# Pairwise products of embedding fields on one core: input loads moved into the store queue, output slots of 116 pairs that cross tile boundaries

## The chip, the cores and the metric

The kernel runs on one core of a Trainium2 chip. The metric is the device time of one execution in microseconds (us); for the kernel before, the median of six runs is 1295.54 us (1290.43 to 1296.54).

## The reference

`x` holds 4096 samples of 32 fields with 64 float32 each, `W` is 64 by 64. Every field is multiplied by `W`, and then every pair of fields i < j gives one vector of 64: the raw field i times the transformed field j. There are 496 pairs.

```python
vid = jnp.einsum('bfd,de->bfe', x, W)
idx_i, idx_j = jnp.triu_indices(32, k=1)
return x[:, idx_i, :] * vid[:, idx_j, :]          # (4096, 496, 64)
```

The input is 33.55 MB and the output 520.09 MB.

## The kernel before

The host lays the samples out so that a tile is 256 samples: 128 partitions (two halves of 128 samples, with 64 embedding elements each) by 32 fields by C = 128 samples. There are NT = 16 tiles. A pair is 128 float32 in each partition, so 512 bytes there and 65,536 bytes over all partitions; a tile gives NP = 496 pairs, and all tiles 7936. In HBM the rows of x are padded by 8 fields (PAD), so that one partition's row of 16 KB stands every 20 KB.

For each tile, TensorE multiplies all fields by W (L134, 16 matmuls of two halves and eight PSUM banks) into `vid`, one PSUM tile of 32 fields that fills all eight banks and is used again by every tile. A matmul into a bank therefore waits until VectorE (DVE in the profile) has read the last tile's fields of that bank. VectorE then forms the pairs with one `tensor_tensor` multiplication for each block of pairs (L159): left the field i from `xt` in SBUF, right the field j from `vid`, result into an output slot `ot`. Tiles 0 and 1 go through the pairs field by field (`by_field`: row j needs only the fields 0 to j), all later tiles by larger blocks (`by_block`).

An output slot holds SLOT = 124 pairs (62 KB in each partition), and a tile is four slots exactly. The pool `opool` has three slots. A slot is stored by one DMA when it is full (L162), except in the first two tiles, where the list GROWING cuts the slots into 26 smaller stores, so that the first ones leave early. VectorE writes into a slot again only when all stores of it have landed.

The input pool `xpool` has two places of 16 KB in each partition. Tile 0 is loaded by four DMAs and tile 1 by two, from the queue of SyncE (SP in the profile). Each later tile t + 1 is loaded during tile t by four DMAs of eight fields (4 KB in each partition), from the queue of ScalarE (ACT in the profile), which does nothing else; it waits until tile t - 1 has been used up. Both queues end in the same 16 DMA engines. SP is scheduled by hand (`manual_schedule`): its DMAs are issued in the order in which the program names them, and a DMA that must wait for VectorE holds up those behind it.

Of the kernel before, what the change touches and what calls it, by code (L numbers as in the profile page):

```python
# [1 line left out]

# [4 lines left out]

F32 = mybir.dt.float32
ALU = mybir.AluOpType

P = 128

C = 128

SLOT = 124

PAD = 8

GROWING = [
    21, 15, 19, 23, 27, 19, 29, 18, 19, 20, 38, 28, 24, 25, 47, 34, 29, 61,  # L20
    55, 69, 66, 58, 77, 47, 93, 31,
]


def by_field():

    return [("row", j, 0, 1, j) for j in range(1, 32)]


def by_block():  # L30


    def within(lo):
        yield "step", lo, 2, 1, 0
        for k in range(2):
            yield "step", lo, 4, 2, k
        for i in (lo, lo + 8):
            yield "row", i + 4, i, 4, 4
        yield "row", lo + 8, lo, 8, 8

    yield from within(0)
    yield "row", 16, 0, 16, 16
    yield from within(16)


def products(blocks):

    at = 0
    for kind, a, b, c, d in blocks:

        if kind == "row":
            rows, n, i0, di, j0, dj = c, d, b, 0, a, 1
        else:
            rows, n, i0, di, j0, dj = 16 // b, c, a, b, a + c + d, b
        r = k = 0
        while r < rows:
            room = SLOT - at % SLOT
            if k or room < n:
                m, w = 1, min(n - k, room)
            else:  # L60
                m, w = min(rows - r, room // n), n
            yield at, m, w, i0 + r * di + k, di, j0 + r * dj, dj
            at += m * w
            if w == n or k + w == n:
                r, k = r + m, 0
            else:
                k += w


def pairs(blocks):  # L70

    for at, m, w, i, di, j, dj in products(blocks):
        for r in range(m):
            for k in range(w):
                yield i + r * di + k, j + r * dj


@with_exitstack
def pairwise_bilinear_kernel(
    ctx: ExitStack,  # L80
    tc: tile.TileContext,
    x: bass.AP,
    w: bass.AP,
    out: bass.AP,
):

    nc = tc.nc  # L90
    NT = x.shape[0]
    F = x.shape[2] - PAD
    D = P // 2
    NP = F * (F - 1) // 2

    BANK = 512 // C


    ctx.enter_context(tc.manual_schedule(engines={mybir.EngineType.SP}))

    const = ctx.enter_context(tc.tile_pool(name="const", bufs=1))
    xpool = ctx.enter_context(tc.tile_pool(name="x", bufs=2))
    opool = ctx.enter_context(tc.tile_pool(name="out", bufs=3))
    psum = ctx.enter_context(
        tc.tile_pool(name="ps", bufs=1, space=bass.MemoryType.PSUM)
    )
    vid = psum.tile([P, F, C], F32)


    w2 = const.tile([P, D], F32)  # L110
    nc.sync.dma_start(out=w2, in_=w)  # L111

    def load(t, pieces, queue):
        xt = xpool.tile([P, F, C], F32, tag="x", name=f"x_{t}")
        n = F // pieces
        for lo in range(0, F, n):
            queue.dma_start(out=xt[:, lo : lo + n, :], in_=x[t][:, lo : lo + n, :])
        return xt

    loaded = [load(0, 4, nc.sync), load(1, 2, nc.sync)]  # L120

    done = 0
    growing = iter(GROWING)
    until = next(growing)
    for t in range(NT):
        if 0 < t < NT - 1:
            loaded.append(load(t + 1, 4, nc.scalar))
        xt = loaded[t]


        for b in range(0, F, BANK):
            for h in range(2):
                half = slice(h * D, (h + 1) * D)
                nc.tensor.matmul(  # L134
                    vid[half, b : b + BANK, :],
                    lhsT=w2[half, :],
                    rhs=xt[half, b : b + BANK, :],
                    start=True,
                    stop=True,
                )  # L140

        sent = 0
        for at, m, w, i, di, j, dj in products(by_field() if t < 2 else by_block()):
            base = at - at % SLOT
            if at == base:
                ot = opool.tile([P, SLOT, C], F32, tag="o", name=f"o_{t}_{at}")
            n = m * w
            o = ot[:, at - base : at - base + n, :]
            if m == 1:
                left = xt[:, i : i + w, :]  # L150
                right = vid[:, j : j + 1, :].to_broadcast([P, w, C])
            else:
                o = o.rearrange("p (m w) c -> p m w c", m=m)
                right = vid[:, j : j + (m - 1) * dj + 1 : dj, :].unsqueeze(2).to_broadcast([P, m, w, C])
                if di == 0:
                    left = xt[:, i : i + w, :].unsqueeze(1).to_broadcast([P, m, w, C])
                else:
                    left = xt.rearrange("p (m d) c -> p m d c", d=di)[:, i // di : i // di + m, i % di : i % di + w, :]
            nc.vector.tensor_tensor(o, left, right, ALU.mult)  # L159
            at += n  # L160
            if t * NP + at == until or at in (base + SLOT, NP):
                nc.sync.dma_start(  # L162
                    out=out[t][:, sent:at, :],
                    in_=ot[:, sent - base : at - base, :],
                )
                sent = at
                if t * NP + at == until:
                    until += next(growing, NT * NP)


_INS = ["r_x", "L0_rec_W"]
_OUTS = [((4096, 496, 64), "float32")]


# [36 lines left out]
```

## Time and profile before

| quantity | value |
|---|---|
| median of six runs | 1295.54 us (1290.43 to 1296.54) |
| the profiled execution: its time, its span | 1290.43 us, 1288.5 us |
| VectorE busy | 1083.6 us, 84%, 320 instructions |
| TensorE busy | 229.2 us, 18%, 512 matmuls |
| DMA packets | 20889, with 553.80 MB, mean 430 GB/s |
| DMAs | 82 stores, 62 loads of x, 1 load of W |

The profiled execution is the fastest of the six runs. 1.93 us of its time lie outside its span. DMA rates in the profile count bytes moved by all 16 engines; a share of the span given for a DMA queue is the time that its packets took, averaged over the 16 engines. The median "to landing" of a DMA runs from its issue to its completion, and so it holds the time it stood behind other DMAs.

### The profile page before, as it was taken

To read this page: it belongs to the slowest core of one execution; us is meant where nothing else is said; L and a number is where in the kernel's file an instruction comes from. 1 tells how busy PE (TensorE), PEld (TensorE's weight loads), DVE (VectorE), ACT (ScalarE), POOL (GpSimd) and SP (SyncE) were. 2 spreads that over 40 slices of the span, in tenths; PEclk is the share of its full clock that TensorE was granted. 3 is DMA by queue.
4 is the path that set the end of the run, shared out by engine and by line. 5 is a ranking of instruction groups with operands and counts; after the bars stand their busy time and mean duration, and the time that the engine had idled before them with its cause. 6 is when DMAs were issued, how large, how long until landed. Compare 5 with 4: busy or idle time off the path is not lost.

```text
span 1288.5 us, 1789 instructions
## 1 busy us (share of the span) xinstructions
PE 229.2 (18%) x512; PEld 48.8 (4%) x512; DVE 1083.6 (84%) x320; POOL 0.2 (0%) x4
## 2 busy tenths in 40 slices
PE   4112122122121121221212212122121221212000
PEld 1000000000000000000000000000000000000000
DVE  7999999898898987988879888798887988979870
POOL 0000000000000000000000000000000000000000
PEclk8555556555555555555555555555555555555555
DMA  9999999999999999999999999999999999999998
GB/s 389 428 428 433 439 434 427 436 436 430 432 435 432 421 435 434 431 434 435 431 436 436 430 436 431 428 434 432 434 425 436 437 436 433 433 429 433 438 434 357
DMA packets 20889, 553.80 MB, mean 430 GB/s; under 512 B 2448, under 2 KB 2448, under 8 KB 10256
## 3 DMA queue, kind: packets, MB, share of 16 engines
q1 hardware_dynamic: 12816, 524.33, 94.2%
q10 hardware_dynamic: 8064, 29.36, 5.6%
q8 instruction: 4, 0.07, 0.0%
q14 instruction: 5, 0.04, 0.0%
HBM read 33.59 MB, written 520.09 MB: 430 GB/s over the span
## 4 chain that ended last, share of the span: by engine, by line
DMA 55%; DVE 40%; issue 2%; PE 0%; DVEq 0%; SPq 0%
DMA out_dram<-o 55%; DVE o L159 40%; DMA x<-in_r_x_dram 0%; PE vid L134 0%; DVEq L200 0%; DVEq L159 0%; SPq L111 0%
## 5 line engine op out<-in xcount | busy, mean ns | idle before, releaser
L159 DVE TENSOR_TENSOR o<-x,vid 128x2048 f32<-128x2048 f32 (+13 forms) x320 | 1083.6, 3453 | 165.1 <-DMA out_dram<-o 120.7
L134 PE MATMUL vid<-x,w 64*64 64x512 f32 x512 | 229.2, 1031 | 952.2 <-DMA x<-in_r_x_dram 624.1
L134 PEld LDWEIGHTS vid<-x,w 64*64 64x64 f32 x512 | 48.8, 206 | 1130.9 <-DVE o L159 588.0
L182 POOL MEMSET const-bfloat16-1.0<- 128x1 bf16 x1 | 0.1, 101 | 0.0
L182 POOL MEMSET const-uint8-127<- 128x1 uint8 x1 | 0.1, 101 | 0.0
L182 POOL MEMSET const-float32-0.0<- 128x1 f32 x1 | 0.1, 98 | 0.2 <-issue 0.2
L182 POOL MEMSET const-float32-1.0<- 128x1 f32 x1 | 0.1, 98 | 0.0
## 6 DMA issues: line engine op xcount, KB each, us to landing
out_dram<-o SPq DMA_DIRECT2D x56, 7936.0 KB, 42.9
x<-in_r_x_dram ACTq DMA_DIRECT2D x56, 512.0 KB, 45.1
out_dram<-o SPq DMA_DIRECT2D x2, 3008.0 KB, 17.7
out_dram<-o SPq DMA_DIRECT2D x1, 5952.0 KB, 26.8
out_dram<-o SPq DMA_DIRECT2D x1, 4928.0 KB, 23.1
out_dram<-o SPq DMA_DIRECT2D x1, 4416.0 KB, 19.0
out_dram<-o SPq DMA_DIRECT2D x1, 4224.0 KB, 21.1
out_dram<-o SPq DMA_DIRECT2D x1, 3904.0 KB, 15.3
```

Of the source, the lines that this page charges most:

```text
L134: nc.tensor.matmul(vid[half, b : b + BANK, :], lhsT=w2[half, :], rhs=xt[half, b : b + BANK, :], start=True, stop=True,)
L159: nc.vector.tensor_tensor(o, left, right, ALU.mult)
L182: nc = _bacc.Bacc("TRN2", target_bir_lowering=False, num_devices=1, dynamic_dma_scratch_size=1024)
```

## The change

Loads. All loads of x are issued from SP, so they stand in one queue with the stores. `xpool` has three places. Before the first tile three tiles are loaded: tile 0 by four DMAs as before, tiles 1 and 2 by one DMA each (16 KB in each partition). After every odd tile (1, 3, ... 13) two more tiles are loaded, one DMA each (one tile after 13). ScalarE's queue is not used any more.

Slots. SLOT is 116 pairs (58 KB in each partition), still three slots. They no longer end with a tile: pairs are counted through all 7936, a slot can hold the last pairs of one tile and the first of the next, and the last slot has 48. GROWING covers the first ten slots with 21 stores, the first of 45 pairs. Blocks are cut at the new slot ends, so VectorE has 363 multiplications for 320.

Layout. The output in HBM was (16 tiles, 128 partitions, 496 pairs, 128), so that one partition's row in a tile stands every 248 KiB; it is now (128 partitions, 7936 + 24 pairs, 128), with a row every 3980 KiB.

```diff
-SLOT = 124
-
-PAD = 8
+SLOT = 116
 
 GROWING = [
-    21, 15, 19, 23, 27, 19, 29, 18, 19, 20, 38, 28, 24, 25, 47, 34, 29, 61,
-    55, 69, 66, 58, 77, 47, 93, 31,
+    45, 46, 25, 55, 61, 44, 72, 58, 58, 77, 39, 87, 29, 76, 40, 90, 26, 33,
+    83, 84, 32,
 ]
+
+XPAD = 8
+OPAD = 24
...
-    xpool = ctx.enter_context(tc.tile_pool(name="x", bufs=2))
+    xpool = ctx.enter_context(tc.tile_pool(name="x", bufs=3))
...
-    def load(t, pieces, queue):
+    loaded = []
+
+    def load(pieces=1):
+        t = len(loaded)
+        if t == NT:
+            return
         xt = xpool.tile([P, F, C], F32, tag="x", name=f"x_{t}")
         n = F // pieces
         for lo in range(0, F, n):
-            queue.dma_start(out=xt[:, lo : lo + n, :], in_=x[t][:, lo : lo + n, :])
-        return xt
-
-    loaded = [load(0, 4, nc.sync), load(1, 2, nc.sync)]
+            nc.sync.dma_start(out=xt[:, lo : lo + n, :], in_=x[t][:, lo : lo + n, :])
+        loaded.append(xt)
+
+    load(4)
+    load()
+    load()
...
     for t in range(NT):
-        if 0 < t < NT - 1:
-            loaded.append(load(t + 1, 4, nc.scalar))
         xt = loaded[t]
...
-        sent = 0
-        for at, m, w, i, di, j, dj in products(by_field() if t < 2 else by_block()):
+        for at, m, w, i, di, j, dj in products(blocks(t), t * NP):
             base = at - at % SLOT
...
-            if t * NP + at == until or at in (base + SLOT, NP):
+            if at == until or at in (base + SLOT, NT * NP):
                 nc.sync.dma_start(
-                    out=out[t][:, sent:at, :],
+                    out=out[:, sent:at, :],
...
+        if t % 2:
+            load()
+            load()
...
-        laid = (NT, 2 * D, shape[1], C)
+        laid = (2 * D, NT * shape[1] + OPAD, C)
```

## The prediction

> **What bounds the kernel now.** I began with the page: the busy shares, the slices and the DMA queues.
>
> ```profile
> PE 229.2 (18%) x512; PEld 48.8 (4%) x512; DVE 1083.6 (84%) x320; POOL 0.2 (0%) x4
> GB/s 389 428 428 433 439 434 427 436 436 430 432 435 432 421 435 434 431 434 435 431 436 436 430 436 431 428 434 432 434 425 436 437 436 433 433 429 433 438 434 357
> q1 hardware_dynamic: 12816, 524.33, 94.2%
> q10 hardware_dynamic: 8064, 29.36, 5.6%
> ```
>
> The two data queues (q1 is SP's, q10 is ACT's, with the 14 later tiles of x) fill 99.8% of the 16 DMA engines' time, and only the first and the last slice lie far below 433 GB/s. So the DMA engines are the bound, and what matters is the engine time that each byte takes. VectorE is next with 1083.6 us: a second bound 205 us away.
>
> Next I read the waits and the chain of waits, to see whether the engines ever lack work.
>
> ```profile
> DVE o L159 <- DMA out_dram<-o: 120.7, 40, 3.5
> DVE o L159 <- issue: 36.4, 12, 3.1
> ...
> 490.86 25.33 DMA out_dram<-o
> ...
> 1131.83 25.10 DMA out_dram<-o
> ```
>
> VectorE waits for a slot to be stored 40 times, about 3 us each (the columns are us in total, times, longest): it is ahead, and two stores stand in the queue whenever it begins a slot. The two chain lines are the same place of the rhythm eight tiles apart: (1131.83 - 490.86) / 8 = 80.12 us for a tile.
>
> Last, the timeline of the final tile and the loads' own rows.
>
> ```profile
> 1194.17 16.75 DVE L159 TENSOR_TENSOR o<-x,vid 128x1536 f32<-128x1536 f32 x2 [1.83 <-DMA out_dram<-o]
> 1212.93 16.75 DVE L159 TENSOR_TENSOR o<-x,vid 128x14336 f32<-128x14336 f32 x2 [2.00 <-DMA out_dram<-o]
> 1231.62 17.07 DVE L159 TENSOR_TENSOR o<-x,vid 128x512 f32<-128x512 f32 x7 [1.94 <-DMA out_dram<-o]
> ...
> L117 ACTq DMA_DIRECT2D x<-in_r_x_dram x56: 334/1246/1468, 76.5 to 1097.5; - x56
> ...
> DMA to landing us min/median/max: 4.0/44.9/81.5
> ```
>
> The last load is issued at 1097.5 and has landed by 1179. After that a slot comes free every (1231.62 - 1194.17) / 2 = 18.73 us: 124 pairs or 8.126 MB, so stores alone run at 433.9 GB/s. Four slots take 74.9 us of a tile's 80.12, which leaves 5.2 us for loading 2.097 MB (403 GB/s). Queue q10 says the same: 5.6% of 1288.5 us over 14 tiles is 5.15 us.
>
> **The change part by part.** The base is this execution, span 1288.5 us and time 1290.43.
>
> Loads with longer rows. At the stores' rate 2.097 MB would take 4.83 us, so a tile's load now has 0.37 us of excess. On each DMA engine such a load is 32 packets of 4 KB and 4 completions, 36 pieces at about 10 ns. After the change it is 8 packets of 16 KB and 1 completion, a quarter: 0.09 us. Saved are 0.28 us x 14 tiles = 3.9 us, all of it on the path, since the engines are the bound. No row shows 16 KB packets in mid-kernel; the nearest are the stores' 62 KB (all excess gone, 5.2 us saved) and the 4 KB loads (nothing saved). I stay near the stores, because their rate, the measure here, already holds 8 packets and 1 completion per engine and DMA, just what the new load has. A loss in this place is the third rival.
>
> The Trainium skill would make far more of it: "DMA: Bandwidth & Descriptors", section "Anatomy of one DMA", fits a transfer from GpSimd as 2.0 us plus its bytes at 436 GB/s, and its rules ask for at least 1 MiB a DMA. By that four loads of 0.524 MB are 12.8 us and one of 2.097 MB is 6.8, an estimate of 84 us over 14 tiles. The trace disagrees, since a whole tile's four loads take 5.2 us of the engines: other transfers fill the latency.
>
> The start. Now three tiles (6.29 MB) come in first. In the first 4 us 0.39 MB move (13 and 184 GB/s in windows of 2 us), worth 0.9 us, so the engines start, in effect, at 3.1 us; at the 428 GB/s below the loads run until 17.8 us. The first store has 45 pairs, rows 1 to 9. VectorE starts row 4 at 9.03, and rows 4 to 9 take 0.68 + 0.81 + 0.95 + 1.08 + 1.21 + 1.34 = 6.1 us, so the store is issued at 15.1, 2.7 us before the loads are through. The first load, issued at 1.16, needed 1.9 us to its start, so the engines stay fed by a margin of 0.8 us; the delay of the first store by 3.8 us costs nothing because tile 2's load fills it. If that cover failed it would cost those 3.8 us.
>
> ```profile
> 4.00:12.00 8.00, 6.69 (x18) 2.25 (x20) 4.06 (x7) 0.00 (x0) 1.00 1.03 428
> 12.00:76.50 64.50, 14.08 (x44) 2.88 (x40) 64.50 (x29) 0.00 (x0) 0.57 1.01 429
> 76.50:213.00 136.50, 28.65 (x62) 5.84 (x64) 135.66 (x52) 0.00 (x0) 0.54 1.01 434
> 1282.00:1288.50 6.50, 0.00 (x0) 0.00 (x0) 0.00 (x0) 0.00 (x0) 0.50 0.11 49
> ```
>
> These are stretches of the span, the last column GB/s. Against 433.9 the first two lose 0.1 and 0.7 us: the many small stores, with VectorE barely keeping pace. With 21 such stores for 26 and 4.8 us more in the queue at the start, I take back half, 0.4 us (0 to 0.8). In all there are 79 stores for 82, so packets per engine go from 656 to 632; that is in this 0.4.
>
> VectorE. 43 more instructions, at a fixed cost of 0.149 us (the 128-element form takes 282 ns, its elements 133): 6.4 us more. They hide behind the 120.7 us in which it waits for stores; without that cover they would cost 6.4 us. A 116-pair slot takes it 15.5 us plus some 0.6 to 1.2, and the two stores ahead hold 2 x 17.5 us, so the engines do not run dry.
>
> SP's order. After an odd tile, SP issues a load into a place long free and a second one into the place of the tile just finished, which waits for VectorE's last product of that tile. Behind it in SP stands the store of the crossing slot, which needs later products anyway, so the wait delays nobody. Two issues add 0.4 us each (SP's store issue takes 0.33), off the path. That store then follows 9.8 us of loads, and VectorE's next free slot comes that much later, once in two tiles, where now it loses 5.2 in each. Data is never late: the new tiles are wanted one and two tiles (80 and 160 us) later, and come after at most two stores, 35 + 10 us. The 36.4 us of "issue" waits at tile starts, where x now comes just in time, should go; nothing follows from it, as what is late next is still the free slot.
>
> The tail. The last store has 48 pairs (7.3 us) behind one of 116, so the queue is again 20 us or more deep when VectorE ends. The last 6.5 us, nearly empty of bytes, stay.
>
> Sum: -3.9 - 0.4 = -4.3 us; span 1284.2, that execution 1286.1. The median of the runs stands 5.1 us above the profiled execution for a reason I can't see; I take it to stay, so 1295.54 - 4.3 = 1291.2 us.
>
> **The rivals.** First, slower by layout. Each partition's rows lay 248 KiB apart and will lie 3980 KiB apart, so the 16 engines write into places spread over 510 MB instead of 32.5 MB. The only layouts that the trace has are 248 KiB (433.9 GB/s) and x's 20 KiB (428): two pitches twelve times apart and no visible effect, but none in the MiB. The stores are 520.09 MB / 433.9 = 1199 us, so each 1% of rate costs 12 us: 1303 us. It decides from 0.6% on, where (4.3 + 2.6) us are lost. Chance 0.12.
>
> The same page, "Latency and other measured facts", warns of this: 4 MiB pitch halves a copy's rate (103 for 207 GB/s) and 4 KiB of padding restores it. 3980 KiB is 116 KiB away from 4 MiB, so by the page nothing is lost; at the halved rate the stores alone would take some 2400 us.
>
> Second, nothing gained. The loads' 403 GB/s may be a price of reading HBM between stores and not of packets. Then only the 0.4 remains: 1295 us. Against it: the first loads run alone at 428 with the same 4 KB rows, though alone they share no engine with stores. Chance 0.21.
>
> Third, slower by switching. In one queue an engine comes to a load straight from a store and could stand until the first byte from HBM, where now the other queue's packets fill that time. There are 7 such places (after tiles 1 to 13). The quickest load lands 4.0 us after issue, 1.2 of them data; if all 2.8 us were exposed each time, 19.6 us, the time would be 1310.8. It decides at (4.3 + 2.6) / 7 = 1.0 us each. Against it: around 12 us, where SP's queue passes from loads to stores, the 2 us windows show 426 and 441 GB/s, no dent, and 32 changes a tile between the queues now cost 0.37 us at most. Chance 0.09.
>
> Fourth, a larger gain: all 5.2 + 0.8 us, and part of the median's 5.1 us if it came from the mixing of reads and writes: 1286. Chance 0.03.
>
> **How the numbers follow.** The forecast has 0.55, its own range 1289.5 to 1293. A measurement of this kernel can tell about 0.2%, 2.6 us, from no change. Faster is the forecast and the fourth, 0.58; the same is the second, 0.21; slower are the first and third, 0.21. The range reaches down to 1284 (the fourth) and up to 1300, where the mild ends of the slower cases lie (0.4% of store rate after the gain, or 1.3 us at each switch), and leaves out their harder ends, some 0.15.
>
> **What would show it.** Right: loads with 8 packets per engine, taking about 4.9 us a tile of queue time; two tiles in 2 x 79.8 us; stores of 116 pairs 17.5 us apart; VectorE busy near 1090 us; first store issued near 15 us with no empty window before it; DMA share at 99% or more. Wrong: slots over 17.7 us apart away from loads (layout), a dent in GB/s after each odd tile (switching), the same 80.1 us a tile (no gain), or an empty stretch before 18 us (the start).

## The result and the profile after

The changed kernel takes 1291.82 us (median of 30 runs, 1291.05 to 1294.08) beside 1296.39 us of the kernel before (60 runs, 1290.43 to 1299.0): a ratio of 0.9972, 95% interval 0.9965 to 0.9979. The forecast was 1291.2, faster by 4.3 us; it is faster by 4.6. The scatter has shrunk too: all 30 runs lie within about 3 us, where those of the kernel before spread over 8.6.

The two profiled executions show the opposite of the medians, 1289.9 us of span for 1288.5, because the first profile had caught the fastest of the 60 executions of the kernel before. So the terms of the sum must be looked for in the rows.

The page after, the DMA slices and the only data queue:

```profile
GB/s 390 439 429 437 426 415 440 438 425 435 432 433 438 437 418 440 425 438 438 425 434 424 440 439 422 438 424 438 437 421 440 427 437 435 426 437 438 424 439 355
q1 hardware_dynamic: 14256, 553.69, 99.7%
```

One queue fills 99.7% of the engines' time, where two had 99.8%: their packets took about 1286 us in both. The slices now go up and down by some 20 GB/s, and the prediction had named dents as the sign of costly change-overs from stores to loads. These dents don't follow the loads: the slice from 1193 to 1225 us, with stores alone, has 424 GB/s, and the one from 967 to 1000 us, with two loads in it, 440. The waits (us in total, times, longest):

```profile
PE vid L142 <- DMA x<-in_r_x_dram: 205.6, 8, 36.1
DVE o L166 <- DMA out_dram<-o: 158.5, 58, 12.8
DVE o L166 <- PE vid L142: 8.3, 2, 7.7
```

VectorE's 36.4 us of "issue" waits are gone. Its waits for stores have become more and longer: 158.5 us in 58 waits for 120.7 in 40, and up to 12.8 us behind two loads. The chain of waits, one stretch of store time with no load in it, one with two loads and one with a single load:

```profile
594.58 36.67 DMA out_dram<-o
...
647.18 47.45 DMA out_dram<-o
...
1100.07 41.48 DMA out_dram<-o
```

Two loads cost the slot that waits behind them 47.45 - 36.67 = 10.8 us, 5.4 each, and the single load after tile 13 costs 4.8. Predicted were 4.9 for each. The timeline of the last tile gives the rhythm of the stores:

```profile
1194.18 15.75 DVE L166 TENSOR_TENSOR o<-x,vid 128x512 f32<-128x512 f32 x3 [1.43 <-DMA out_dram<-o]
1211.72 15.69 DVE L166 TENSOR_TENSOR o<-x,vid 128x14336 f32<-128x14336 f32 x2 [1.78 <-DMA out_dram<-o]
1229.21 16.07 DVE L166 TENSOR_TENSOR o<-x,vid 128x1536 f32<-128x1536 f32 x8 [1.81 <-DMA out_dram<-o]
```

A slot of 116 pairs every 17.5 us: 7.602 MB at 434 GB/s, the old rate. Neither loads nor stores have become faster. What has?

### The profile page after: what moved, and what is told of

Its sections match the earlier page's. It is cut to its first block, busy times and chain, and to the rows that moved or that the text cites. A ratio compares the mean times of both kernels' runs of the same rounds, so it can differ in the third digit from the quotient of the medians.

```text
span 1289.9 us, 1722 instructions
## 1 busy us (share of the span) xinstructions
PE 217.3 (17%) x512; PEld 43.8 (3%) x512; DVE 1086.8 (84%) x363; POOL 0.2 (0%) x4
## 3 DMA queue, kind: packets, MB, share of 16 engines
q1 hardware_dynamic: 14256, 553.69, 99.7%
## 4 chain that ended last, share of the span: by engine, by line
DMA 62%; DVE 33%; issue 2%; PE 0%; DVEq 0%; SPq 0%
DMA out_dram<-o 61%; DVE o L166 33%; DMA x<-in_r_x_dram 0%; PE vid L142 0%; DVEq L166 0%; SPq L114 0%
## 5 line engine op out<-in xcount | busy, mean ns | idle before, releaser
L166 DVE TENSOR_TENSOR o<-x,vid 128x1024 f32<-128x1024 f32 (+18 forms) x363 | 1086.8, 3061 | 166.8 <-DMA out_dram<-o 158.5
L142 PE MATMUL vid<-x,w 64*64 64x512 f32 x512 | 217.3, 980 | 963.7 <-DVE o L166 758.2
L142 PEld LDWEIGHTS vid<-x,w 64*64 64x64 f32 x512 | 43.8, 198 | 1135.5 <-DVE o L166 872.4
```

The costliest lines, as they stand in the source:

```text
L142: nc.tensor.matmul(vid[half, b : b + BANK, :], lhsT=w2[half, :], rhs=xt[half, b : b + BANK, :], start=True, stop=True,)
```

## The experiments

The theories: **P**, the prediction's, says that fewer and longer packets make the loads cheaper. **E**, formed after the first four runs, supposes that the 16 DMA engines each have a fixed share of every DMA and never wait for one another, that some fall behind while loads run among stores, and that the last one ends the kernel. In the trace each DMA has 16 packets of 4 bytes, taken here as the completions of the 16 engines, so those of the last store tell how far apart the engines finish. The time from the first to the last of them is called the spread below; the "lead" is how long before the last engine an engine ends, in the mean over the 16; "work" is the time of all packets of the data queues divided by 16. The other theories' letters are explained in the expectations. All times are in us.

| kernel | median us | ratio to before (95%) | span of its profile | work | spread | lead |
|---|---|---|---|---|---|---|
| before, first profile | 1296.39 | | 1288.5 | 1285.8 | 4.9 | 3.1 |
| before again | 1296.22 | 0.9999 (0.9985 to 1.0014) | 1294.8 | 1287.0 | 11.4 | 8.5 |
| changed | 1291.82 | 0.9972 (0.9965 to 0.9979) | 1289.9 | 1285.4 | 5.5 | 3.4 |
| before, 16 KB loads | 1306.80 | 1.0068 (1.0044 to 1.0092) | 1305.5 | 1291.6 | 18.6 | 13.0 |
| before, loads in SP's queue | 1302.22 | 1.0040 (1.0021 to 1.0059) | 1300.3 | 1288.3 | 15.1 | 10.9 |
| before, new layout | 1296.08 | 0.9994 (0.9979 to 1.0009) | 1289.3 | 1285.8 | 5.7 | 4.0 |
| changed, one load at a time | 1297.95 | 1.0020 (1.0008 to 1.0032) | 1297.0 | 1286.6 | 12.8 | 9.3 |
| changed, three at a time | 1291.67 | 0.9964 (0.9951 to 0.9976) | 1290.0 | 1285.4 | 5.5 | 3.7 |
| changed, loads from ACT | 1290.70 | 0.9959 (0.9945 to 0.9972) | 1289.2 | 1285.3 | 6.2 | 4.3 |
| same, one at a time | 1291.30 | 0.9976 (0.9964 to 0.9988) | 1288.2 | 1285.6 | 5.2 | 3.0 |
| slots alone | 1296.01 | 1.0007 (0.9996 to 1.0019) | 1294.1 | 1286.1 | 8.1 | 6.1 |
| slots alone, early store | 1296.28 | 1.0007 (0.9998 to 1.0015) | 1294.0 | 1286.9 | 8.0 | 5.6 |
| changed, 4 KB loads | 1292.49 | 0.9971 (0.9960 to 0.9982) | 1291.6 | 1287.4 | 6.7 | 4.4 |
| changed, no later loads | 1224.11 | 0.9445 (0.9432 to 0.9458) | 1222.0 | 1219.7 | 1.5 | 0.9 |

Each ratio is to runs of the kernel before on the same chip at the same time; the medians of the kernel before in these groups were 1294.6 to 1296.8.

**The kernel before, once more.** The edit is one dead line:

```diff
-    done = 0
```

> The kernel before once more, without its dead line 'done = 0'. The time must be the same, near 1296 us. What is looked for is a second profile, because the first one caught an execution 6 us under the median. Theory P (the prediction's): the 6 us lie around the kernel or are spread evenly, and a tile's load still costs 5.2 us of queue time. Theory Q (two queues beside one another): the usual execution differs from the fast one in the stretches where loads run; a two-tile period of over 160.2 us, or engines that finish at different times.

The same time, 1296.22, and a profile near the median, span 1294.8. Its queues, and its last stretches (the last column is GB/s):

```profile
q1 hardware_dynamic: 12816, 524.33, 93.8%
q10 hardware_dynamic: 8064, 29.36, 5.5%
```

```profile
1280.00:1282.00 2.00, 0.00 (x0) 0.00 (x0) 0.00 (x0) 0.00 (x0) 0.50 0.81 349
1282.00:1284.00 2.00, 0.00 (x0) 0.00 (x0) 0.00 (x0) 0.00 (x0) 0.50 0.37 159
1284.00:1286.00 2.00, 0.00 (x0) 0.00 (x0) 0.00 (x0) 0.00 (x0) 0.50 0.37 159
1286.00:1288.00 2.00, 0.00 (x0) 0.00 (x0) 0.00 (x0) 0.00 (x0) 0.50 0.15 63
1288.00:1290.00 2.00, 0.00 (x0) 0.00 (x0) 0.00 (x0) 0.00 (x0) 0.50 0.22 95
1290.00:1292.00 2.00, 0.00 (x0) 0.00 (x0) 0.00 (x0) 0.00 (x0) 0.50 0.07 32
```

and the same stretches of the changed kernel:

```profile
1280.00:1282.00 2.00, 0.00 (x0) 0.00 (x0) 0.00 (x0) 0.00 (x0) 0.50 0.86 369
1282.00:1284.00 2.00, 0.00 (x0) 0.00 (x0) 0.00 (x0) 0.00 (x0) 0.50 0.77 332
1284.00:1286.00 2.00, 0.00 (x0) 0.00 (x0) 0.00 (x0) 0.00 (x0) 0.50 0.40 172
1286.00:1288.00 2.00, 0.00 (x0) 0.00 (x0) 0.00 (x0) 0.00 (x0) 0.50 0.26 111
1288.00:1290.00 2.00, 0.00 (x0) 0.00 (x0) 0.00 (x0) 0.00 (x0) 0.50 0.00 0
```

and of the kernel before in its first profile:

```profile
1280.00:1282.00 2.00, 0.00 (x0) 0.00 (x0) 0.00 (x0) 0.00 (x0) 0.50 1.02 444
1282.00:1284.00 2.00, 0.00 (x0) 0.00 (x0) 0.00 (x0) 0.00 (x0) 0.50 0.30 127
1284.00:1286.00 2.00, 0.00 (x0) 0.00 (x0) 0.00 (x0) 0.00 (x0) 0.50 0.07 32
```

In the usual execution of the kernel before, the packets fill 1287.0 of 1294.8 us, 99.4% instead of 99.8%, and the bytes run out over ten microseconds, from 1282 to 1292, where in the first profile they do so within four. Eight of the last store's 16 completions lie within 0.2 us; the other eight are spread over the next 11. The work per engine is the same within 1.2 us. So the 5.1 us that the prediction could not see are the wait for the last engine: the lead is 8.5 us for 3.1. The tile's period is longer too, as theory Q asked. The same place of the chain eight tiles apart,

```profile
491.00 26.17 DMA out_dram<-o
...
1138.17 25.19 DMA out_dram<-o
```

gives (1138.17 - 491.00) / 8 = 80.9 us for 80.1: by theory E, the pace of an engine that lags.

**16 KB loads on ACT's queue.**

```diff
-            loaded.append(load(t + 1, 4, nc.scalar))
+            loaded.append(load(t + 1, 1, nc.scalar))
```

> The kernel before, with one DMA for each later tile of x instead of four, still on ScalarE's queue: 16 KB packets, nothing else. Theory P (fewer packets and completions make the load cheaper): 3.9 us faster than before, near 1292. Theory Q (the single queue is what gains): 1296, no change beyond 2 us. If reads cost more as longer bursts: slower.

Some 9 to 10 us slower, which neither P nor Q had; only the third possibility named before the run did, without a number. P alone is refuted by this: the packets got longer and the kernel slower. The load packets themselves took their 611 ns (4 KB: 159 ns), but the packets of the stores took 8.8 us per engine more than in the first profile of before (1208.8 us for 1200.0), and the engines ended unevenly:

```profile
1284.00:1288.00 4.00, 0.00 (x0) 0.00 (x0) 0.00 (x0) 0.00 (x0) 0.50 0.59 254
1288.00:1292.00 4.00, 0.00 (x0) 0.00 (x0) 0.00 (x0) 0.00 (x0) 0.50 0.40 175
1292.00:1296.00 4.00, 0.00 (x0) 0.00 (x0) 0.00 (x0) 0.00 (x0) 0.50 0.26 111
1296.00:1300.00 4.00, 0.00 (x0) 0.00 (x0) 0.00 (x0) 0.00 (x0) 0.50 0.18 79
```

For 16 us fewer and fewer engines work.

**The queue alone.**

```diff
-    loaded = [load(0, 4, nc.sync), load(1, 2, nc.sync)]
+    loaded = [load(0, 4, nc.sync), load(1, 1, nc.sync)]
...
-        if 0 < t < NT - 1:
-            loaded.append(load(t + 1, 4, nc.scalar))
...
+        if t + 2 < NT:
+            loaded.append(load(t + 2, 1, nc.sync))
```

> The kernel before, with its slots of 124 pairs, its layout and its two places for x, but each later tile of x loaded by one DMA in SP's queue, right behind the last store of the tile whose place it takes. Theory P: 3.9 us faster, 1292, as it too has 16 KB packets. Theory Q: it has the whole gain of the change, 1291 to 1292, and as narrow a spread of times. Theory S (each change-over from stores to a load costs 1.2 us in one queue): 14 change-overs for 7, so 5 to 8 us behind the changed kernel, about 1298.

Slower by 5.7 us than the kernel before and by 10.4 than the changed one, against P and Q: the single queue is not what gains. S had the direction, but its 5 to 8 us behind the changed kernel were too few. The spread is 15.1 us, and in the trace it grows with nearly every load.

**The layout alone.**

```diff
-                    out=out[t][:, sent:at, :],
+                    out=out[:, t * NP + sent : t * NP + at, :],
...
-        laid = (NT, 2 * D, shape[1], C)
+        laid = (2 * D, NT * shape[1] + 24, C)
```

> The kernel before with the changed kernel's output layout alone (rows every 3980 KiB instead of 248 KiB). Prediction: no effect, 1296 within 2 us. The layout rival: slower, 12 us for each 1% of store rate. If the layout is where the gain comes from: 1291 to 1292.

No effect, 1296.08: the first rival falls. Its profile was again of an even execution, spread 5.7, span 1289.3.

**One load at a time.**

```diff
-        if t % 2:
-            load()
-            load()
+        load()
```

> The changed kernel with one load after every tile instead of two after every odd one: same queue, same 16 KB packets, same slots and layout, but 13 change-overs from stores to loads instead of 7. Theory E (evenness: in each change-over some of the 16 DMA engines lose 0.5 to 1.1 us more than others, they never wait for one another, and the last one ends the kernel): the spread of the engines' last completions grows from 5.5 us to 9 to 14, and the time by as much, 1296 to 1300. Theory C (slots that cross tiles and the third place make the gain): unchanged, 1292.

6.1 us slower than the changed kernel, spread 12.8, as E said and C not. Its queue is busy for less of the span, with the same packets:

```profile
q1 hardware_dynamic: 14256, 553.69, 99.2%
```

**Three at a time.**

```diff
-SLOT = 116
+SLOT = 105
...
-    xpool = ctx.enter_context(tc.tile_pool(name="x", bufs=3))
+    xpool = ctx.enter_context(tc.tile_pool(name="x", bufs=4))
...
-        if t % 2:
-            load()
-            load()
+        if t % 3 == 2:
+            for _ in range(3):
+                load()
```

> The changed kernel with loads of three tiles at a time: four places for x, four tiles loaded first, 4 change-overs; to make room, slots of 105 pairs, with the early stores cut to suit them. Theory E: the spread falls to about 3 us and the time by 2 to 3 us against the changed kernel, to 1289 to 1290. Theory C, or smaller stores costing something: 1292 or above (about 7 more DMAs of 8 packets; at 10 ns for each packet 0.5 us).

1291.67, no gain over the changed kernel and a spread of 5.5: E's number is missed. So the spread is not simply a count of change-overs. Here it crept up among the stores as well, by 1.2 us after the last loads.

**The changed kernel without its later loads** (what is left out stands in the expectation).

```diff
-        xt = loaded[t]
+        xt = loaded[t % 3]
...
-        if t % 2:
-            load()
-            load()
```

> The changed kernel with no loads after the first three tiles: all later tiles compute from those three (left out: 13 loads, 27.3 MB; the products are of the wrong tiles). Packets of 16 KB at 611 ns, 8 to an engine and load, are 63.6 us. Theory E: those and the 4.5 us that the spread had grown in the 7 change-overs, so 68 us less, 1224, with a spread of 1 to 2 us. If the change-overs cost every engine the same and evenness is nothing: 13 x 5.4 = 70 us less with the spread still at 5. The prediction's 4.9 us a load: 64 us less, 1228.

1224.11, on E's number: 67.7 us less, 63.5 of them the packets' own time. The spread never exceeds 2.6 us and ends at 1.5, so nearly all of the unevenness comes with loads among the stores, and stores alone add little.

**The loads back on ACT's queue, two at a time, and one at a time.**

```diff
-    def load(pieces=1):
+    def load(pieces=1, queue=nc.sync):
...
-            nc.sync.dma_start(out=xt[:, lo : lo + n, :], in_=x[t][:, lo : lo + n, :])
+            queue.dma_start(out=xt[:, lo : lo + n, :], in_=x[t][:, lo : lo + n, :])
...
-            load()
-            load()
+            load(4, nc.scalar)
+            load(4, nc.scalar)
```

> The changed kernel with its later tiles loaded as before the change, by four DMAs each (4 KB packets) on ScalarE's queue, two tiles at a time; slots, places and layout stay changed. Theory E: spread and time as of the kernel before, between 1293 and 1298, with a wide scatter from run to run. Theory C: 1292 with a narrow scatter.

1290.70, within 1.5 us for all runs. E expected the old time and scatter and was wrong; C was right that the move into SP's queue is not needed. Its queues:

```profile
q1 hardware_dynamic: 12384, 526.42, 94.5%
q10 hardware_dynamic: 7488, 27.27, 5.2%
```

Together 99.7%, as in the changed kernel. This version is 1.1 us below the changed one, but the two intervals overlap. The second kernel has `load(4, nc.scalar)` after every tile:

> The run with ScalarE's queue again (slots and layout of the changed kernel, three places, 4 KB packets), but one tile loaded after each tile instead of two after each odd tile. The number of 4 KB packets among the stores is the same. Theory T: 1290 to 1291, as with two. Theory N (what counts is the number of times that loading starts, as it did in SP's queue, where one at a time cost 6 us): 1294 to 1297.

1291.30, close to T's 1290 to 1291 and far from N's range: in a queue of their own it made no difference clear of noise whether one or two tiles were loaded at a time.

**Slots alone.** The changed kernel with two places for x and the old loads:

```diff
-    xpool = ctx.enter_context(tc.tile_pool(name="x", bufs=3))
+    xpool = ctx.enter_context(tc.tile_pool(name="x", bufs=2))
...
-    load()
-    load()
+    load(2)
...
+        if 0 < t < NT - 1:
+            load(4, nc.scalar)
         xt = loaded[t]
```

> The slot part of the change alone: slots of 116 pairs that cross tiles, the new early stores and layout, but two places for x and loads as before the change (tile 1 by two DMAs, each later tile by four on ScalarE's queue during the tile in front of it). Theory T (with loads of 4 KB packets on their own queue, the new slots are what keeps the 16 engines even): 1290 to 1292 with a narrow scatter, a last spread of 5 to 6 us. Theory L (the third place and the time at which loads are issued are what does it): 1296 with a wide scatter, as before, spread 5 to 11 us from run to run.

1296.01 with a spread of 8.1: no gain, as L said, though with a narrow scatter. Part of it is the start, where two tiles no longer fill the time until the first store of 45 pairs. First this kernel, then the changed one:

```profile
12.00:20.00 8.00, 5.47 (x26) 1.47 (x22) 8.00 (x7) 0.00 (x0) 1.00 0.75 318
```

```profile
12.00:20.00 8.00, 6.00 (x28) 1.72 (x24) 8.00 (x7) 0.00 (x0) 1.00 1.01 429
```

(434 - 318) / 434 x 8 = 2.1 us are lost there. The slots may gain as much elsewhere: in the usual execution of the kernel before the lead is 8.5 us, and here it is 6.1 (one profile each). Would an earlier store mend it?

```diff
-    45, 46, 25, 55, 61, 44, 72, 58, 58, 77, 39, 87, 29, 76, 40, 90, 26, 33,
+    21, 24, 46, 25, 55, 61, 44, 72, 58, 58, 77, 39, 87, 29, 76, 40, 90, 26, 33,
```

> The slot part alone again, with its first store of 45 pairs cut into 21 and 24, so that stores begin when they did before the change. In the run without this cut the first slice of the span fell from 389 to 359 GB/s, worth 32.3 us x 30 / 434 = 2.2 us. If that is the start without the third tile's cover: 2.2 us faster than that run, 1293.8, the first slice near 389, and the rest of the gap to the changed kernel (2 us) is the engines' spread, which should stay near 8 us. If the start is not it: 1296.

It does not: 1296.28. The hole moves, to 371 GB/s from 20 to 32 us, 1.7 us:

```profile
20.00:32.00 12.00, 1.97 (x4) 0.29 (x4) 12.00 (x8) 0.00 (x0) 0.50 0.87 371
```

In both cuts tried the engines run ahead of VectorE's short rows. The kernel before, with two tiles in front as well but smaller early stores (21, 15, 19 and 23 pairs), has no such hole, 428 GB/s from 12 to 20 us and 433 from 20 to 32. So the third tile makes good what the new list of stores would cost; against the kernel before, the start gains nothing.

**4 KB loads in SP's queue.**

```diff
-            load()
-            load()
+            load(4)
+            load(4)
```

> The changed kernel with each of its 13 later loads cut into four DMAs of 4 KB packets, in the same queue and at the same places: the prediction's main term by itself. Prediction (excess paid by the packet and the completion): a quarter of 0.37 us becomes 0.37 us again, 0.28 x 13 = 3.6 us slower than the changed kernel, 1295.4. By the packets' own durations (159 ns for 4 KB, 611 ns for 16 KB, 9 ns a completion): 32 x 159 - 8 x 611 + 3 x 9 = 227 ns a load, 3.0 us slower, 1294.8. If the cost of a change-over grows with the length of the rows behind it: the same or faster, 1292 or below, with a smaller spread.

1292.49, 0.7 us slower than the changed kernel by the medians and level with it by the ratios to before (0.9971 and 0.9972), where the prediction's term was 3.6. By packets the engines' work rose by 2.0 us and not by the nominal 3.0, since the later loads' packets took less time beyond their usual 159 and 611 ns: 2.6 us for 4.0.

## Why the prediction was right, and where it was not

The time, the direction and the range were right; the step behind nine tenths of the gain was not. That the number came out as forecast is luck: a saving that didn't come was replaced by one that the prediction had taken to be nothing.

**Loads with longer rows, -3.9 us: the step that failed.** The size of the excess was nearly right: a 4 KB packet takes 159 ns where the stores' rate would give 151, a 16 KB packet 611 for 604, a completion 9, so nominally 14 loads save about 3 us. But in the changed kernel load packets average 644 ns. It is not the first ones behind the stores that are long: from the second pair on, the first quarter of each group of loads by time takes 611 ns a packet, and nearly all of the excess, 2.5 of 2.8 us per engine, lies in the last quarter, where packets of up to 1.7 us run beside packets of the next stores. All loads of x took 83.1 us of each engine, for 82.0 before: the term of -3.9 us measured +1.1. The third rival's cost was real, though the long packets are not the first behind a store, as it supposed: in four of the five pairs in the chain of waits, a pair of loads holds the slots up by 1.1 to 1.3 us more than its bytes at the stores' rate (in the fifth by 0.3), just above the 1.0 us from which it was said to decide. The kernel came out faster all the same, by what its end gained.

**The tail, "stays", and the median's 5.1 us, "I take it to stay".** Here the time came from. Against the usual execution of the kernel before, the span fell by 1294.8 - 1289.9 = 4.9 us, and the lead, the mean time for which an engine has nothing left to do while the last one works, by 8.5 - 3.4 = 5.1. The sum of the packets' times fell by 1.6 us (stores 2.3 less, loads 1.1 more, the rest completions), but some records overlap, up to 21 at once for 16 engines; between the idle times at the start and at the end, the engines are at work for 1283 us in both. So the even end is the whole gain. This is one pair of profiles, though over the 13 profiles with all loads the span is long where the lead is. The prediction read the engines' busy share as one number, and from a profile with an unusually even end. Its fourth rival, with a chance of 0.03, came nearest to the source: part of these 5.1 us, from the mixing of reads and writes.

**The start** was right: the first store is issued at 15.09 us (15.1), and no window before it is empty. That tile 2's load is the cover showed when it was taken away, at 2.1 us for the 3.8 stated. **VectorE** was right: 1086.8 us for "near 1090", and its 43 instructions cost nothing. **SP's order** was right: its loads wait 35.3 us for VectorE in all. TensorE waits 205.6 us for loaded data, but VectorE waits only 8.3 us for TensorE, so it costs nothing that shows. **Layout**: right, no effect (ratio 0.9994), though 128 rows of 3980 KiB span 522 MB and not 510. The Trainium skill's page "DMA: Bandwidth & Descriptors", section "Latency and other measured facts", has half the rate for copies at a pitch of 4 MiB. No run here tried 4 MiB; at 3980 KiB the stores kept 434 GB/s.

**What in the change brings the gain.** Not the queue: with the loads in SP's queue one at a time both kernels get 6 us slower, and with loads on ACT's queue the changed one is as fast or faster. Not the layout, and not the slots alone, which lose 2.1 us at the start and leave the time as it was. The third place for x, with the tile loaded ahead that it allows, makes the difference between 1296.0 (slots alone) and 1291.3 (loads from ACT, one at a time): 2.1 us at the start, and 3.1 in the lead (6.1 to 3.0). Loading in pairs keeps SP's queue from spoiling it. The slots of 116 pairs give up 12 of the 16 KB in each partition that the third place takes. No run had the third place with the old slots, so how much of the evenness needs both isn't known.

**Still open**: why loads with 4 KB packets on ACT's queue leave the engines more even with three places than with two, when they run for about the same share of the time (5.2% and 5.5%), and which engines lag. The packets' records name no engine, and the spread of the kernel before varies from run to run by itself (4.9 and 11.4 us in its two profiles).

## What to carry to other kernels

When the DMA engines are over 99% busy, compare their mean work with the span and look at the last 10 us in windows of 2: the gap, 2.3 to 14.0 us in the profiles here, is mostly the wait for the slowest engine, and here it grew mainly where loads ran among stores. Terms of 0.3% can't be read from one profiled execution; profile a kernel twice, and take the one near the median. Moving the loads into the store queue saved nothing by itself here. One more place for x did, and in the store queue it did so only with the loads in groups.

## What the runs showed of the hardware

Packet durations are very regular: the medians are 159, 611, 2192 and 2342 ns for 4, 16, 58 and 62 KB, so beyond 4 KB a packet's length hardly matters (25 ns for four small ones against one large). What surprised is what neighbours do: with 16 KB loads on a second queue beside 62 KB stores, the stores' packets took 8.8 us per engine more than with 4 KB loads in the same place (1208.8 for 1200.0), and the engines ended 18.6 us apart. And little evens the engines out: with stores running two deep, the changed kernel's spread, once at 5.9 us, still ended at 5.5, and without loads it took 770 us to fall from 2.6 to 1.5.
